# Two of a pack's four hat products moved from the second burst to the end of the first burst's turn, in a two-layer convolution kernel

## The chip, the core and the metric

The kernel runs on one core of one Trainium2 chip. A core has TensorE (PE in the profile; its weight loads are PEld), VectorE (DVE), ScalarE (ACT), GpSimd (POOL) and SyncE (SP), which here only issues DMAs. The metric is the device time of one execution in microseconds. Three executions of the kernel before gave 12756.01, 12768.52 and 12776.53 us; the median, 12768.52 us, is the time before.

## What is computed

The input is a batch of 32 images with 128 channels of 32 x 32 pixels. Layer 0 normalizes, encodes to 1024 channels, convolves along the flattened pixels, gates, normalizes and decodes. Layer 1 is a deformable depthwise convolution with 8 x 8 taps: a small depthwise convolution gives an offset for each tap and pixel, and the image is sampled there with bilinear weights.

```python
x = x + L0(_gn(x))            # h = u@W_enc; y = gelu(conv(h)); g = y@W_glu
                              # layernorm(h + g[:D]*sigmoid(g[D:])) @ W_dec
x = x + L1(_gn(x))
# L1, for each of 64 taps:
ix = px * sx - 0.5; iy = py * sy - 0.5
s = ((1-dx)*(1-dy))*gather(y0, x0) + (dx*(1-dy))*gather(y0, x0+1) \
  + ((1-dx)*dy)*gather(y0+1, x0) + (dx*dy)*gather(y0+1, x0+1)
acc = acc + s * w_t
# then batch norm and gelu
```

## The kernel before

A first stage makes the convolution of layer 0 for all images and leaves y in HBM. The main stage, `main_block`, then runs two generators side by side. `first_part(b)` does gate, values, normalization and decoding of layer 0 for one image, as two halves of 512 pixels with eight blocks m each: eight matmuls for the gate (L808), a sigmoid on ScalarE (L815), eight matmuls for the value (L831), the gating on VectorE (L839), one matmul of h (L847), a sum on VectorE (L860), its square on ScalarE (L868), and sums on GpSimd (L738, L869). `second_part(b)` does layer 1 for an image that is two behind. `run_along` merges them: it always advances the one that has done the smaller share of its cost, so that instructions of the two interleave in a fixed order on every engine. `prepare(b + 1)` is a list of steps with due times for the next image of layer 1 (normalization, depthwise taps, laying out of offsets in HBM), which `second_part` works off in `due(j)`: a step runs when its due time is at most three times the piece number plus j.

Bilinear sampling is done as a matmul. The hat function max(0, 1 - |t|) of an offset along x, times that along y, gives the weights of a small window of pixels (tile `s`, ds in the profile, 16 slots of 160 columns), and TensorE multiplies windows of the image (dxw) with them. An image has 17 packs of tap columns. For a pack h:

- the x hats of the whole image were made by `prepare` and stored in HBM; `load_x` brings those of a pack into one of two ds buffers (L1110), at the end of pack h - 2;
- the y offsets of a half pack come by `load_y` (L1125) into one of three dhy buffers, four DMAs in most packs;
- `hat_y(h, part)` makes the y hats of a quarter of a pack in place, two ScalarE instructions (L1145, L1146);
- `weights(h, part)` multiplies a quarter of ds by it on VectorE, 128 x 640 in most packs (L1151); after parts 1 and 3 it issues the `load_y` that reuses the buffer.

A pack's matmuls go in two bursts, pieces 0 and 1 (i = 0) and pieces 2 and 3 (i = 2), into four PSUM banks (dps, L1227). After each burst VectorE multiplies the banks by the tap weights into `prod`, one bank in each of four slots ("a turn", L1243), and at the end of the pack GpSimd adds up (L1269, L1275). A burst has six slots, which the `yield` lines bound: one after the matmuls, four with a bank each, one after `due(5)`. So a pack has twelve.

The products of pack h + 1 stand ahead of the second burst of pack h, and its hats in the first burst's turn. [...]SyncE's queue holds all loads of both streams: y of layer 0 (gy, L728), windows (dxw, L1166), the copies of `prepare` (L972, L984, L999, L1046), and those named above. `spread` (L984) copies offsets from HBM to HBM in runs of 20 values, four times an image.

Of the kernel before, what the change touches and what calls it, by code (L numbers as in the profile page):

```python
# [589 lines left out]
def main_block(nc, tc, const, ins, x, u_d, y_d, x1_d, out, offmax):  # L590
# [21 lines left out]
    with ctx:  # L612
# [459 lines left out]
        packs = [(b, us) for b in range(B) for _, us in PACKS]  # L1072
        s_of, hy_of, xw_of = {}, {}, {}

        def slots_of(n):
            return sum(span_of(u)[1] for u in PACKS[n][1])
# [56 lines left out]
        PARTS = 4  # L1133

        def cut_of(h, part):

            ends = ends_of(h)
            lo, hi, first = ends[part], ends[part + 1], ends[part - part % 2]
            t = hy_of[2 * h + part // 2]
            return slice(lo, hi), t[:, lo - first : hi - first]  # L1140

        def hat_y(h, part):

            t = cut_of(h, part)[1]
            nc.scalar.activation(t, t, AF.Abs, bias=minus_y)  # L1145
            nc.scalar.activation(t, t, AF.Relu, scale=-1.0, bias=const["one"])  # L1146

        def weights(h, part):

            cut, t = cut_of(h, part)  # L1150
            nc.vector.tensor_mul(s_of[h][:, cut], s_of[h][:, cut], t)  # L1151
            if part % 2:
                q = 2 * h + part // 2
                hy_of.pop(q)
                load_y(q + HB)
# [15 lines left out]
        def second_part(b, steps):  # L1171


            steps = sorted([*steps, *ending], key=lambda e: e[0])
            ending.clear()
            acc = one.tile([P, W, H], F32, tag="acc", name=f"dacc_{b}")
            nc.gpsimd.memset(acc, 0.0)
            for n in range(NP):
                x0, us = PACKS[n]
                m = slots_of(n)  # L1180
                xw = xw_of[b, x0]
                windows(b, n + 1)
                prod = prods[(b * NP + n) % 2]

                h = b * NP + n
                s = s_of.pop(h)

                for i in range(0, PIECES, 2):

                    def due(j):  # L1190
                        while steps and steps[0][0] <= 3 * (PIECES * n + i) + j:
                            steps.pop(0)[1]()

                    due(0)
                    work = []
                    if i > 0 and h + 1 < len(packs):
                        for part in range(PARTS):
                            weights(h + 1, part)
                    for piece in (i, i + 1):
                        ps = [  # L1200
                            psam.tile(
                                [P, 512], F32, tag="sam", name=f"dps_{b}_{n}_{piece}_{side}"
                            )
                            for side in range(2)
                        ]
                        lo = 0
                        for parts in zip(blocks_of(0, piece), blocks_of(1, piece)):
                            rows, run = parts[0][0][1], parts[0][0][3]
                            hi = lo + rows * run * m
                            to = [  # L1210
                                t[:, lo:hi].rearrange("p (s k v) -> p s k v", s=m, k=rows)
                                for t in ps
                            ]
                            for part in range(len(parts[0][1])):
                                for side in range(2):
                                    (ky, _, v0, _, step, skew), wins = parts[side]
                                    w, r0, r1 = wins[part]
                                    half = slice(64 * side, 64 * side + 64)
                                    frm = s[half, 0, ky * NV + v0 - VBASE[side] + r0 :]
                                    frm = bass.AP(  # L1220
                                        tensor=frm.tensor, offset=frm.offset,
                                        ap=[
                                            frm.ap[0], [CELLS, m],
                                            [step * NV + skew, rows], [1, r1 - r0],
                                        ],
                                    )
                                    nc.tensor.matmul(  # L1227
                                        to[side][:, :, :, r0:r1],
                                        xw[half, w, :], frm, start=True, stop=True,
                                    )  # L1230
                            for side in range(2):
                                work.append((piece, side, to[side], parts[side][0]))
                            lo = hi
                    yield measure(m)

                    def scale(piece, side):
                        for p, sd, frm, (ky, rows, v0, run, step, skew) in work:
                            if (p, sd) != (piece, side):
                                continue
                            wt = wk[:, table_of[n] : table_of[n] + m]  # L1240
                            wt = wt[:, :, ky : ky + step * (rows - 1) + 1 : step]
                            at_y = prod[:, ky * KS + v0 - ky :]
                            nc.vector.tensor_mul(  # L1243
                                bass.AP(
                                    tensor=at_y.tensor, offset=at_y.offset,
                                    ap=[
                                        at_y.ap[0], [H, m],
                                        [step * (KS - 1) + skew, rows], [1, run],
                                    ],
                                ),  # L1250
                                frm,
                                wt[:, :, :, None].to_broadcast([P, m, rows, run]),
                            )

                    for j in range(4):
                        due(1 + j)
                        scale(i + j // 2, j % 2)
                        if i == 0 and h + 1 < len(packs):
                            hat_y(h + 1, j)
                        yield measure(m)  # L1260
                    due(5)
                    yield measure(m)
                load_x(h + SB)

                def row(ky):
                    return prod[:, ky * KS : ky * KS + m * H]

                for to, frm in ((2, 0), (3, 1), (4, 6), (5, 7), (2, 4), (3, 5), (2, 3)):
                    nc.gpsimd.tensor_add(row(to), row(to), row(frm))  # L1269
                total = row(2)  # L1270
                slot = 0
                for u in us:
                    j0, nj = span_of(u)
                    to = acc[:, u - 7 + j0 : u - 7 + j0 + nj]
                    nc.gpsimd.tensor_add(  # L1275
                        to, to,
                        total[:, slot * H : (slot + nj) * H].rearrange(
                            "p (s y) -> p s y", y=H
                        ),
                    )  # L1280
                    slot += nj

            o = two.tile([P, L], F32, tag="img", name=f"do_{b}")
            xr = two.tile([P, L], F32, tag="img", name=f"dxr_{b}")
            nc.sync.dma_start(xr, x1_d[b])
            nc.gpsimd.tensor_scalar(  # L1286
                o.rearrange("p (h w) -> p w h", w=W), acc, bn_mean, bn_inv,
                op0=ALU.subtract, op1=ALU.mult,
            )
            ending.append((6, lambda: nc.scalar.activation(o, o, AF.Gelu, bias=bn_beta)))  # L1290
            ending.append((11, lambda: nc.vector.tensor_add(o, o, xr)))
            ending.append((14, lambda: nc.scalar.dma_start(out[b], o)))

        ending = []
        def measure(slots):

            return slots * 8.0 + 40.0
# [3 lines left out]
        def opening():  # L1301

            yield 30.0
            for _, step in prepare(0):
                step()
                yield 1.0
            for i in range(SB):
                load_x(i)
            for i in range(HB):
                load_y(i)  # L1310
            windows(0, 0)
            for part in range(PARTS):
                hat_y(0, part)
                weights(0, part)


        ctx.enter_context(tc.manual_schedule())
# [158 lines left out]
```

## Time and profile before

| what | value |
|---|---|
| time, median of three (lowest to highest) | 12768.52 us (12756.01 to 12776.53) |
| profiled execution: time, span | 12769.27 us, 12767.5 us |
| granted TensorE clock, mean | 0.972 |
| dps matmuls (L1227) | 23936 records, 2778.3 us busy |
| ds products (L1151) | 2176, 2821.2 us busy |
| y hats (L1145, L1146) | 2176 each, 1699.1 and 1726.5 us busy |
| dhy loads of 160 KB (L1125) | 3264 of about 4030 |
| ds loads of 400 KB or 480 KB (L1110) | 832 and 448 |

Times in the views are microseconds from the start of the span. A row of waits names the engine and line that waited, what ended the wait, the total, how often, and the longest. A row of the timeline gives start, duration, engine, line and operation, with "xN" for N instructions merged. The chain of waits is followed back from the end: each piece is the work that released the next one. Matmul records come in pairs: each matmul of 32-bit data shows as two.

### The profile page before, as it was taken

To read this page: it belongs to the slowest core of one execution; us is meant where nothing else is said; L and a number is where in the kernel's file an instruction comes from. 1 tells how busy PE (TensorE), PEld (TensorE's weight loads), DVE (VectorE), ACT (ScalarE), POOL (GpSimd) and SP (SyncE) were. 2 spreads that over 40 slices of the span, in tenths; PEclk is the share of its full clock that TensorE was granted. 3 is DMA by queue.
4 is the path that set the end of the run, shared out by engine and by line. 5 is a ranking of instruction groups with operands and counts; after the bars stand their busy time and mean duration, and the time that the engine had idled before them with its cause. 6 is when DMAs were issued, how large, how long until landed. Compare 5 with 4: busy or idle time off the path is not lost.

```text
span 12767.5 us, 157327 instructions
## 1 busy us (share of the span) xinstructions
PE 12216.4 (96%) x51362; PEld 6679.5 (52%) x51362; DVE 8277.2 (65%) x14315; ACT 5490.5 (43%) x7823; POOL 8094.1 (63%) x6987
## 2 busy tenths in 40 slices
PE   7999999999999999999999999999999999999965
PEld 7999444444444444444444444444444444444444
DVE  5555126666666667666666666666666666666667
ACT  4344124444444444444444444444444444444443
POOL 2555126666666676666666666667666666666668
PEclk9999999999999999999999999999999999999976
DMA  7899136666666666667666776666666667667666
GB/s 238 268 278 276 68 90 177 181 181 186 180 183 181 179 176 183 182 175 184 183 181 177 186 187 180 178 176 173 183 181 176 184 176 186 180 183 187 179 183 180
DMA packets 1521915, 2350.16 MB, mean 184 GB/s; under 512 B 619586, under 2 KB 835266, under 8 KB 1520066
## 3 DMA queue, kind: packets, MB, share of 16 engines
q1 hardware_dynamic: 1382210, 2027.97, 60.4%
q10 hardware_dynamic: 89728, 177.76, 3.8%
q0 software_dynamic: 49152, 134.28, 3.5%
q8 instruction: 413, 6.77, 0.2%
q14 instruction: 412, 3.38, 0.1%
HBM read 2016.61 MB, written 407.02 MB: 190 GB/s over the span
## 4 chain that ended last, share of the span: by engine, by line
PE 78%; DMA 7%; DVE 5%; POOL 3%; issue 2%; ACT 2%; SPq 2%; ACTq 0%; DVEq 0%; POOLq 0%
PE gpv L831 24%; PE gpg L808 23%; PE dps L1227 16%; PE psy L320 5%; PE psz L237 3%; DMA ds<-dhat 3%; PE gpo L736 3%; PE gph L847 3%; DVE ds L1151 2%; DVE prod L1243 2%; POOL prod L1269 1%; DMA dhy<-rel_d 1%; SPq L1125 1%; POOL do L1286 1%; DMA dxw<-dxw_d 1%
## 5 line engine op out<-in xcount | busy, mean ns | idle before, releaser
L1269 POOL TENSOR_TENSOR prod<-prod 128x512 f32<-128x512 f32 (+3 forms) x3808 | 4994.8, 1343 | 1614.0 <-DVE prod L1243 1571.4
L1243 DVE TENSOR_TENSOR prod<-dps,k_weight_slots 128x512 f32<-128x512 f32 (+16 forms) x8704 | 3126.1, 408 | 1437.5 <-PE dps L1227 1128.2
L808 PE MATMUL gpg<-gy,g_w_glu 128*128 128x512 f32 x8192 | 3771.8, 603 | 41.0 <-ACT gs L815 27.0
L831 PE MATMUL gpv<-gy,g_w_glu 128*128 128x512 f32 x8192 | 3751.7, 600 | 0.0
L1151 DVE TENSOR_TENSOR ds<-ds,dhy 128x640 f32<-128x640 f32 (+2 forms) x2176 | 2821.2, 1342 | 620.7 <-DMA ds<-dhat 354.8
L1227 PE MATMUL dps<-ds,dxw 64*128 64x128 f32 (+14 forms) x23936 | 2778.3, 375 | 364.4 <-DVE prod L1243 329.5
L1227 PEld LDWEIGHTS dps<-ds,dxw 64*128 64x128 f32 x23936 | 1979.9, 197 | 1455.5 <-DVE prod L1243 560.5
L808 PEld LDWEIGHTS gpg<-gy,g_w_glu 128*128 128x128 f32 x8192 | 1522.7, 191 | 1965.0 <-issue 1910.6
L831 PEld LDWEIGHTS gpv<-gy,g_w_glu 128*128 128x128 f32 x8192 | 1514.0, 190 | 1887.3 <-issue 1887.3
L869 POOL TENSOR_TENSOR gs<-gs,gq 128x512 f32<-128x512 f32 x448 | 647.2, 1445 | 2257.2 <-ACT gq L868 2257.2
L1145 ACT ACTIVATE dhy<-dhy,k_minus_y 128x640 f32<-128x640 f32 (+2 forms) x2176 | 1699.1, 781 | 532.5 <-DMA dhy<-rel_d 197.7
L1146 ACT ACTIVATE dhy<-dhy,one 128x640 f32<-128x640 f32 (+2 forms) x2176 | 1726.5, 793 | 71.1
L868 ACT ACTIVATE gq<-gr 128x512 f32<-128x512 f32 x448 | 281.4, 628 | 2556.9 <-DVE gr L860 2555.6
L839 DVE SCALAR_TENSOR_TENSOR gs<-gpv,k_b_glu,gs 128x512 f32<-128x512 f32 x512 | 384.2, 750 | 1374.8 <-PE gpv L831 1296.9
L815 ACT ACTIVATE gs<-gpg,k_b_glu 128x512 f32<-128x512 f32 x512 | 351.6, 687 | 1867.3 <-PE gpg L808 1722.0
L1275 POOL TENSOR_TENSOR dacc<-dacc,prod 128x256 f32<-128x256 f32 (+6 forms) x1184 | 1048.1, 885 | 92.8
L357 POOL DMA_DIRECT2D y_d<-yo x1024 | 590.0, 583 | 690.6 <-ACT yo L344 641.2
L320 PE MATMUL psy<-toe,z 128*128 128x192 f32 x4096 | 668.0, 326 | 7.4 <-DVE z L242 5.5
L320 PEld LDWEIGHTS psy<-toe,z 128*128 128x128 f32 x4096 | 663.3, 196 | 11.4 <-DVE z L242 6.8
L738 POOL TENSOR_TENSOR gs<-gs,gr 128x512 f32<-128x512 f32 x448 | 652.3, 1456 | 0.0
L335 DVE TENSOR_TENSOR psy<-psy,t 128x256 f32<-128x256 f32 (+2 forms) x768 | 333.8, 435 | 345.9 <-ACT t L328 329.1
L847 PE MATMUL gph<-gu,k_W_enc 128*128 128x512 f32 x1024 | 522.9, 592 | 0.0
(164 smaller groups left out, 6046.8 us busy)
## 6 DMA issues: line engine op xcount, KB each, us to landing
dhy<-rel_d SPq DMA_DIRECT2D x3264, 160.0 KB
ds<-dhat SPq DMA_DIRECT2D x832, 400.0 KB
ds<-dhat SPq DMA_DIRECT2D x448, 480.0 KB
dxw<-dxw_d SPq DMA_DIRECT2D x832, 224.0 KB
y_d<-yo POOLq DMA_DIRECT2D x1024, 128.0 KB, 4.1
gy<-y_d SPq DMA_DIRECT2D x512, 256.0 KB
u<-u_d SPq DMA_DIRECT2D x224, 512.0 KB
dhat<-dh ACTq DMA_DIRECT2D x256, 390.0 KB
```

What stands on the lines that cost most here:

```text
L320: nc.tensor.matmul(ps[:, c // 2, c % 2, :], rows[i][:, (g * CG + c0 + c) // 2, c % 2, :], toe[:, c0 + c, :], start=True, stop=True,)
L738: nc.gpsimd.tensor_add(sums[0], sums[0], r)
L808: nc.tensor.matmul(gate, w_glu[:, k, D + m * P : D + m * P + P], ys[k], start=(k == 0), stop=(k == KD - 1),)
L831: nc.tensor.matmul(val, w_glu[:, k, m * P : m * P + P], ys[k], start=(k == 0), stop=(k == KD - 1),)
L847: nc.tensor.matmul(h, w_enc[:, m * P : (m + 1) * P], u, start=True, stop=True)
L1145: nc.scalar.activation(t, t, AF.Abs, bias=minus_y)
L1146: nc.scalar.activation(t, t, AF.Relu, scale=-1.0, bias=const["one"])
L1151: nc.vector.tensor_mul(s_of[h][:, cut], s_of[h][:, cut], t)
L1227: nc.tensor.matmul(to[side][:, :, :, r0:r1], xw[half, w, :], frm, start=True, stop=True,)
L1243: nc.vector.tensor_mul(bass.AP(tensor=at_y.tensor, offset=at_y.offset, ap=[at_y.ap[0], [H, m], [step * (KS - 1) + skew, rows], [1, run],], ...
L1269: nc.gpsimd.tensor_add(row(to), row(to), row(frm))
L1275: nc.gpsimd.tensor_add(to, to, total[:, slot * H : (slot + nj) * H].rearrange("p (s y) -> p s y", y=H),)
```

## The change

Products 0 and 1 of pack h + 1 stand at the end of the first burst's turn in pack h, after `due(5)` and ahead of the last slot; products 2 and 3 stay ahead of the second burst. Hats 2 and 3 of pack h + 1 go into the first two slots with a bank of the first turn, and hats 0 and 1 of pack h + 2 into the same slots of the second turn. The opening makes hats 0 and 1 of pack 1 too. As `weights(h + 1, 1)` issues a `load_y`, that load moves with it.

```diff
                     due(0)
                     work = []
                     if i > 0 and h + 1 < len(packs):
-                        for part in range(PARTS):
-                            weights(h + 1, part)
+                        weights(h + 1, 2)
+                        weights(h + 1, 3)
                     for piece in (i, i + 1):
...
                     for j in range(4):
                         due(1 + j)
                         scale(i + j // 2, j % 2)
-                        if i == 0 and h + 1 < len(packs):
-                            hat_y(h + 1, j)
+                        if j < 2 and h + 1 + i // 2 < len(packs):
+                            hat_y(h + 1 + i // 2, (2, 0)[i // 2] + j)
                         yield measure(m)
                     due(5)
+                    if i == 0 and h + 1 < len(packs):
+                        weights(h + 1, 0)
+                        weights(h + 1, 1)
                     yield measure(m)
                 load_x(h + SB)
...
             for part in range(PARTS):
                 hat_y(0, part)
                 weights(0, part)
+            for part in range(2):
+                hat_y(1, part)
```

## The prediction

> **What bounds the kernel now.** I read four views of the profile, from coarse to fine. First, busy time by stretch: the convolution stage, the main stage in which both parts of the block run together, and the tail in which the last two images have the deformable part alone (rows: stretch and length, then busy us of PE, PEld, DVE, ACT, POOL, the granted clock, DMA share, GB/s).
>
> ```profile
> PE 12216.4 (96%) x51362; PEld 6679.5 (52%) x51362; DVE 8277.2 (65%) x14315; ACT 5490.5 (43%) x7823; POOL 8094.1 (63%) x6987
> ...
> 1853.00:12212.00 10359.00, 10223.34 (x40281) 5058.19 (x40281) 7059.68 (x12082) 4625.43 (x6177) 7002.17 (x5563) 0.99 0.68 180
> 12212.00:12767.00 555.00, 291.08 (x1555) 219.87 (x1553) 395.44 (x716) 232.04 (x300) 417.25 (x336) 0.64 0.69 187
> ```
>
> In the main stage TensorE stands still for 10359.0 - 10223.3 = 135.7 us, over 30 images 4.5 us each. That is all a better order can win there, with some clock: 0.99 instead of 1.00 is about 1% of 10223, another 100 us. The tail is 555 us, and TensorE is busy for 291 of it. Second, who ended TensorE's waits, in these two stretches (us, times, longest):
>
> ```profile
> PE dps L1227 <- DVE prod L1243: 124.1, 88, 7.2
> PE dps L1227 <- DMA dhy<-rel_d: 6.9, 1, 6.9
> PE dps L1227 <- DMA dxw<-dxw_d: 4.7, 1, 4.7
> ...
> PE dps L1227 <- DVE prod L1243: 205.4, 36, 18.5
> ```
>
> So it is always a burst's bank that VectorE has not yet read out. Third, VectorE's own waits in the main stage: what holds it where it should make the next pack's weights (ds)?
>
> ```profile
> DVE ds L1151 <- DMA ds<-dhat: 289.7, 148, 6.5
> DVE do L1291 <- ACT do L1290: 170.9, 29, 6.3
> DVE ds L1151 <- ACT dhy L1146: 168.1, 97, 2.9
> ...
> DVE gn_r L917 <- ACT gn_r L914: 90.2, 30, 3.0
> ```
>
> Fourth, one image's stalls. There are two that count. One of about 0.7 us (5076.6 to 5077.3, say) is VectorE at its limit among the depthwise taps: 19.2 of 20 us busy. The other comes 54 us later, in packs 8 and 9, and takes 1.2 to 7.2 us. Here it is in the chain of waits, 6157 to 6177 us:
>
> ```profile
> 6157.54 5.57 DMA dhy<-rel_d
> 6163.10 0.02 issue
> 6163.12 8.90 DMA ds<-dhat
> 6172.02 0.03 DVEq L1151
> ...
> 6172.84 0.82 DVE ds L1151
> 6173.66 0.35 DVE prod L1243
> 6174.01 0.04 issue
> 6174.05 3.48 PE dps L1227 x24
> 6177.53 3.03 PE gpg L808 x4
> ```
>
> TensorE's first burst of pack 9 waits for a bank; VectorE has the products of pack 9's weights ahead of the evictions, and these wait for the last piece of the load into ds. That load was issued late because SyncE and the DMA engines were at the spreads (rel_d, 80-byte runs):
>
> ```profile
> 6139.47 10.36 SPq L984 DMA_DIRECT2D rel_d<-rel_n  x3
> 6149.93 8.85 SPq L1125 DMA_DIRECT2D dhy<-rel_d  x8
> 6158.87 2.68 SPq L728 DMA_DIRECT2D gy<-y_d  x4
> 6161.82 1.83 SPq L1110 DMA_DIRECT2D ds<-dhat  x3
> ```
>
> From 6140 to 6174 the DMA share is 0.97. The end of the stall is the landing of the third piece (6172.02), two products of 0.82 and an eviction. In the tail it is a loop through the same load: products, dhy loads, ds load, landing, about 14.1 us a pack (products of successive packs start at 12570.84, 12585.30 and 12599.11).
>
> **What the Trainium skill says.** "PSUM — Partial Sum Buffer", section Engine vs sequencer instructions: the queues of ScalarE, VectorE and GpSimd are strictly first in, first out. The trace fits: VectorE ends its sum (L860) at 5020.50 and then sits 3.03 us before L917, with products behind it whose load had landed. So what matters is which neighbours an instruction passes. "SBUF — State Buffer", Who interferes with whom: a VectorE instruction with two SBUF inputs contends with a GpSimd one that reads SBUF. A 128x640 product takes 1.361 us on average but 0.82 in the stall, where GpSimd waits too; moving products doesn't take that cost off. "DMA: Bandwidth & Descriptors", Issuing engines are not separate DMA queues: all DMAs end on the same 16 engines; only the issuing time differs by place. In the window above this decides. "TensorE: Matmul & The Clock Gate", What's actually happening: an idle array is throttled and must be busy again before it runs at full rate. Here, after 2.34 us of idling, four gate records took 3.03 us instead of 1.72, so an idle us costs about another.
>
> **The change, part by part.** I laid the instruction sequences of the two programs side by side.
>
> TensorE and GpSimd: no instruction changes place. Nothing is added or dropped on any engine: 2176 products, 2176 pairs of hat functions, the same loads.
>
> VectorE: the move sounds large and is small. Between the end of the first turn and the second burst lies one slot of the other stream. An image has 17 x 12 = 204 slots beside 292 matmul slots, so 1.43 matmuls a slot; eight records take 3.43 us, two records a matmul, so 0.86 us each and 1.2 us a slot. A VectorE instruction of the other stream rarely falls into it. In fact only 61 pairs of products pass anything: 31 pass L917/L918 (pack 3) and 30 pass L860 (pack 8), so two places an image.
> - Pack 3: VectorE waited 90.2/30 = 3.0 us for ACT's square root; two products, 2 x 1.36 = 2.7 us, now fill it. TensorE was busy 20.00 of 20 us there, and VectorE had caught up by 5035.09, where it waits 0.82 us for TensorE. Worth 0 in the main stage, at best 30 x 0.7 = 21 us if the following stall went with it.
> - Pack 8: in the old order L860 runs at 6165.21, and the products start at 6168.48 and 6170.09. In the new one the second product ends at 6170.92, L860 until 6171.67, still before the third piece lands at 6172.02. Worth 0; if it doesn't fit, 0.75 x 30 = 22 us lost. Behind L860 wait ACT's square (L868) and GpSimd's sums; the matmuls that need these (L736 at 6180.40, the mean's later) are not reached.
>
> ScalarE: the hat pairs keep their own sequence, parts 0, 1, 2, 3 pack after pack. Parts 0 and 1 move six slots earlier against the sigmoids and squares, parts 2 and 3 two slots. A pair is 0.817 + 0.829 = 1.65 us. VectorE's 168.1 us of waiting for hats should nearly vanish, but it is not where TensorE stalls (packs 8 and 9 wait for the load), so I cost it at 0. What covers it is TensorE's other work; without that it would be up to 168 us. The earlier places of parts 2 and 3 ask for their dhy load 2 slots sooner: normally it is issued at 5001.5 and used after 5012; in pack 8 ScalarE will wait some 2 us, with L868 as the next instruction and its input later still. 0 again.
>
> SyncE: in each pack four dhy loads go out one slot earlier. In sequence they pass one window copy (L1046) twice an image, one gy load, and, in pack 7, the last of the four spreads. The last is the place that counts. The spread now goes behind four dhy issues of 0.64 us, 2.6 us. The four move from behind to before it, so all from the fifth dhy on stands behind the same work as before. With the DMA share at 0.97 I expect the ds load to land at the same time: 0. Bounds: 2.6 us later, if issuing decides, and 1 us earlier, as the last dhy load need not wait for the spread (at 10321.56 it did so for 1.0 us). Both are per image and count twice for the clock.
>
> The tail: order as before but for image 31's preparation. The two products before L917 save about 3 us of its chain (products started at 12288.44, behind L918 and a hat that is gone from that place), and the ds load after the spreads is issued perhaps 2 us sooner. -5 us. The opening does two hat pairs more, 3.3 us, under image 1's matmuls, and pack 0 does them less: 0.
>
> Sum: 0 + 0 + 0 + 0 - 5 = -5 us against the profiled execution's 12769.27 us (span 12767.5), which is 0.8 us over the median of the three runs. So 12764 us: no change that can be measured (0.2%, 26 us, is what I take as the bound).
>
> **The rivals.**
> - A, faster: the congested stretch drains sooner. For it: small and large runs get mixed, and the digits of DMA share between 6147 and 6158 fall to 0.6, so the DMA engines are not full while spreads are generated. Against: the total is the same and the ds load keeps its place. If the load lands 1 us sooner: 30 x 1 x 2 = 60, 12709 us.
> - B, slower: SyncE becomes what decides in pack 7. The four dhy loads wait for VectorE's second product, and the last spread, all other loads and the ds load wait behind. It decides once the ds load's issue slips more than the queue hides: by the semaphore updates in the trace, a piece of ds takes 6.5 us (median) from issue to landing, 3.9 at least, so 2.6 us. I price half the upper bound: 30 x 1.3 x 2 = 78, 12847 us. Against: the slip equals the cover at worst.
> - C: hats that wait for dhy hold a sigmoid (L815), and TensorE runs out of its three gate banks. For it: in the main stage L839 waited 60.3 us behind hats already. 30 x 0.7 = 21 us, 12790.
>
> **How the numbers follow.** Forecast 0.58, A 0.26, B 0.11, C 0.05. The forecast's own range, 12742 to 12790, has both pack places' bounds. To leave out no more than 2 in 10 I reach over A's middle and to C: 12705 to 12800. Faster: A's greater part and a little of the forecast, 0.25; slower: B and part of C, 0.15; same 0.60.
>
> **What would show it.** Right: VectorE's wait for hats under 40 us, that for ACT in L917 near 0, TensorE's idle time in the main stage still 120 to 150 us, the pack 9 stall ending with a ds landing. Wrong: that stall gone or doubled, the ds load issued over 2 us later after the spreads, or waits of L808 and L831 for ACT.

## The result, and the profile after

| | before | after |
|---|---|---|
| median (lowest to highest), 20 runs each on one chip | 12767.22 us (12750.74 to 12780.0) | 12787.56 us (12769.97 to 12802.37) |
| ratio, 95% interval | | 1.0017 (1.001 to 1.0024) |
| profiled execution: time, span | 12769.27, 12767.5 us | 12774.51, 12772.8 us |

The change made the kernel slower by about 20 us, 0.17%, where -5 us had been forecast. The profiled execution of the changed kernel is one of the quickest of its twenty, so its trace shows only 5 us of that. In the text below "before" and "after" are these two traces.

Busy time by stretch, of after, for the main stage and the tail (columns as in the prediction):

```profile
1853.00:12212.00 10359.00, 10224.28 (x40285) 5066.05 (x40283) 7073.43 (x12072) 4630.81 (x6172) 6973.98 (x5559) 0.99 0.69 180
12212.00:12767.00 555.00, 296.14 (x1568) 226.17 (x1564) 405.10 (x727) 232.83 (x302) 420.88 (x340) 0.63 0.70 187
```

Taken alone this says that nothing happened: TensorE stands still for 10359.0 - 10224.3 = 134.7 us, against 135.7. TensorE's waits of after in the main stage:

```profile
PE dps L1227 <- DVE prod L1243: 96.8, 53, 6.7
PE dps L1227 <- DMA dhy<-rel_d: 34.1, 6, 7.4
```

The sum is 130.9 us (135.7 in three rows before), but there are 59 waits where there were 90. The short ones are gone and the long ones are longer. VectorE's waits of after, in the same stretch:

```profile
DVE ds L1151 <- DMA ds<-dhat: 255.3, 135, 7.0
...
DVE ds L1151 <- ACT dhy L1146: 6.5, 6, 2.0
```

The wait for y hats went from 168.1 us to 6.5, and the one in L917 (90.2 us) no longer appears. Next the place where TensorE stalls, in the same image as the prediction's stall at 6172 us; in after it comes some 14 us later in the span. This is the timeline of after there, first VectorE (start, duration, instruction, and in brackets the idle time before it), then GpSimd:

```profile
6182.79 0.82 DVE L1151 TENSOR_TENSOR ds<-ds,dhy 128x640 f32<-128x640 f32 x1 [4.18 <-DMA ds<-dhat]
6184.48 0.83 DVE L1151 TENSOR_TENSOR ds<-ds,dhy 128x640 f32<-128x640 f32 x1 [0.86 <-DMA ds<-dhat]
6185.22 0.75 DVE L860 SCALAR_TENSOR_TENSOR gr<-gph,k_b_enc,gs 128x512 f32<-128x512 f32 x1
6186.87 2.52 DVE L1151 TENSOR_TENSOR ds<-ds,dhy 128x640 f32<-128x640 f32 x2 [0.91 <-ACT gq L868]
```

```profile
6186.71 1.27 POOL L869 TENSOR_TENSOR gs<-gs,gq 128x512 f32<-128x512 f32 x1 [9.47 <-ACT gq L868]
```

This is the new thing. The third piece of ds landed at 6186.79 (by the semaphore updates in the trace). The last pair of products starts 0.08 us later, and its row takes 2.52 us. In before the row of the same pair takes 1.56 us (VectorE, then GpSimd):

```profile
6165.21 0.75 DVE L860 SCALAR_TENSOR_TENSOR gr<-gph,k_b_enc,gs 128x512 f32<-128x512 f32 x1
...
6172.10 1.56 DVE L1151 TENSOR_TENSOR ds<-ds,dhy 128x640 f32<-128x640 f32 x2 [1.19 <-DMA ds<-dhat]
```

```profile
6166.70 1.26 POOL L869 TENSOR_TENSOR gs<-gs,gq 128x512 f32<-128x512 f32 x1 [2.97 <-ACT gq L868]
```

GpSimd adds a square to its sum here (L869). In before this addition is over at 6167.96, ahead of all four products; in after it falls into the 2.52 us. It does so because L860 now stands behind the first pair of products and runs later: L860 releases ScalarE's square (L868), and that releases the addition, 1.49 us after L860 began. The bracket on the last row names ScalarE, but the product waited for the load; the square merely ended at about the same time. The chain of waits of after errs in the same way:

```profile
6179.13 9.45 DMA gy<-y_d
...
6188.58 0.81 DVE ds L1151
6189.39 0.34 DVE prod L1243
...
6189.78 4.95 PE dps L1227 x24
```

It sees only the last product and credits the time before it to whatever transfer ended nearest, a gy load that no product needs. A product that runs slowly looks like a wait for something else; its duration in the timeline tells the truth. The last row has a second lesson, taken up below: 24 records took 4.95 us, where the same group in before's chain took 3.48.

SyncE's issues of after in this image (start, time, line, transfer):

```profile
6152.52 7.14 SPq L984 DMA_DIRECT2D rel_d<-rel_n  x2
6161.98 3.96 SPq L1125 DMA_DIRECT2D dhy<-rel_d  x4
6165.98 0.59 SPq L984 DMA_DIRECT2D rel_d<-rel_n  x1
6166.67 5.67 SPq L1125 DMA_DIRECT2D dhy<-rel_d  x4
...
6174.90 2.83 SPq L1110 DMA_DIRECT2D ds<-dhat  x3
```

The last spread stands between the two groups of dhy loads now, as the diff says. To see what this adds up to I took means over images from the traces, each image counted from its first gate matmul (L808) to that of the next:

| mean over 29 images, us | before | after |
|---|---|---|
| short stall at the depthwise taps | 0.79 | 0.18 |
| first spread issued | 141.83 | 140.69 |
| last spread issued | 153.51 | 158.26 |
| third ds piece lands | 180.53 | 179.18 |
| end of the long stall | 182.58 | 182.11 |
| landing to end of stall | 2.05 | 2.93 |
| long stall | 3.50 | 4.22 |

The landing comes 1.35 us earlier, and 0.88 us of that is lost between landing and matmul.

### The profile page after: what moved, and what is told of

It reads as the page before. It is cut to its first block, busy times and chain, and to the rows that moved or that the text cites. A ratio compares the mean times of both kernels' runs of the same rounds, so it can differ in the third digit from the quotient of the medians.

```text
span 12772.8 us, 157357 instructions
## 1 busy us (share of the span) xinstructions
PE 12217.9 (96%) x51362; PEld 6691.2 (52%) x51362; DVE 8298.8 (65%) x14315; ACT 5499.2 (43%) x7823; POOL 8069.5 (63%) x6987
## 4 chain that ended last, share of the span: by engine, by line
PE 72%; DVE 9%; DMA 9%; issue 3%; POOL 3%; SPq 3%; ACT 1%; ACTq 0%; DVEq 0%; POOLq 0%
PE gpv L831 23%; PE gpg L808 21%; PE dps L1227 15%; PE psy L320 5%; DVE ds L1151 4%; PE psz L237 3%; DMA ds<-dhat 3%; PE gpo L736 3%; PE gph L847 3%; DVE prod L1243 2%; DMA dxw<-dxw_d 2%; DMA dhy<-rel_d 2%; POOL prod L1272 1%; SPq L1125 1%; POOL do L1289 1%
## 5 line engine op out<-in xcount | busy, mean ns | idle before, releaser
L808 PE MATMUL gpg<-gy,g_w_glu 128*128 128x512 f32 x8192 | 3775.1, 604 | 43.7 <-ACT gs L815 29.3
L1151 DVE TENSOR_TENSOR ds<-ds,dhy 128x640 f32<-128x640 f32 (+2 forms) x2176 | 2882.0, 1375 | 410.9 <-DMA ds<-dhat 321.7
L808 PEld LDWEIGHTS gpg<-gy,g_w_glu 128*128 128x128 f32 x8192 | 1523.0, 191 | 1971.6 <-issue 1901.3
L869 POOL TENSOR_TENSOR gs<-gs,gq 128x512 f32<-128x512 f32 x448 | 659.9, 1473 | 2327.8 <-ACT gq L868 2327.7
L868 ACT ACTIVATE gq<-gr 128x512 f32<-128x512 f32 x448 | 281.4, 628 | 2857.3 <-DVE gr L860 2856.1
L839 DVE SCALAR_TENSOR_TENSOR gs<-gpv,k_b_glu,gs 128x512 f32<-128x512 f32 x512 | 384.2, 750 | 1468.1 <-PE gpv L831 1448.4
L847 PE MATMUL gph<-gu,k_W_enc 128*128 128x512 f32 x1024 | 522.9, 592 | 0.0
```

Of the source, the lines that this page charges most:

```text
L808: nc.tensor.matmul(gate, w_glu[:, k, D + m * P : D + m * P + P], ys[k], start=(k == 0), stop=(k == KD - 1),)
L847: nc.tensor.matmul(h, w_enc[:, m * P : (m + 1) * P], u, start=True, stop=True)
L869: nc.gpsimd.tensor_add(sums[1], sums[1], sq)
```

## The experiments

Theory P (port): pack 3's fill is worth something, as everything up to the ds landing comes over 1 us earlier, and pack 8's move costs about 0.9 us an image, because it sends GpSimd's sum into the pair of products that ends the stall. "The pair" below is these last two products of pack 9, after the third piece has landed; its times are means over images that count each product alone (1.65 us in before, 2.52 in after). Rivals: S, SyncE's order in pack 7 makes the load late; H, ScalarE's hats are in the way; G, the chain of loads gives back whatever VectorE gains. The experiments ran on four chips, A to D, and on A and B all kernels are some 90 us slower than on the chip of the result. Each ratio is against runs of the kernel before on the same chip.

**Chip A (kernel before: 12859.65 us).** The changed kernel again:

> The changed kernel once more, for a second trace. P (GpSimd in the way): in the traces so far VectorE's two products after the last ds piece has landed take 1.65 us together before the change and 2.52 us after it, because GpSimd's sum L869, which the sum L860 sets off, now runs beside them. P expects the same here: 2.3 to 2.7 us for the pair, the end of the stall 2.9 us after the landing (2.05 before the change), stall near 4.2 us an image or longer, stall of the depthwise taps near 0.2 us; time 1.0017 of before. S (SyncE's order in pack 7) expects instead that the ds load of pack 9 lands later after the first spread than before the change (38.7 us): 39 us or more in a run as slow as the median. H (ScalarE's hats) expects waits of TensorE or VectorE on ScalarE that weren't there.

12852.77 us, ratio 0.9998 (0.9990 to 1.0006). The pair took 2.56 us, and the stall ended 2.97 us after the landing, as P says. The ratio that I expected was missed: on this chip the change costs nothing. That became the second question.

Pack 8 left as it was:

```diff
-                        weights(h + 1, 2)
-                        weights(h + 1, 3)
+                        for part in range((0 if n == 8 else 2), PARTS):
+                            weights(h + 1, part)
...
-                        weights(h + 1, 0)
-                        weights(h + 1, 1)
+                        for part in range((0 if n == 8 else 2)):
+                            weights(h + 1, part)
```

> The change in every pack but pack 8, where all four products stay ahead of the second burst, so that L860 is ahead of them again. P: the pair of products back at 1.65 us, end of the stall 2.05 us after the landing; the landing stays early (1.3 us earlier in the image than before the change, from pack 3). Some 0.9 us an image less than the changed kernel, and with the clock 27 to 42 us: 0.9985 to 1.0000 of before, the stall near 3.3 us. S and H: nothing but pack 8's order has changed, so as the changed kernel, 1.0017, stall 4.2 us.

12829.63 us, 0.9977 (0.9970 to 0.9984), 23 us less than the changed kernel. Pair 1.65 us, end of stall 2.05 us after the landing. S and H are against this: nothing of theirs, pack 7's issues and the hats, was touched.

The kernel before with pack 3 alone, and with pack 8 alone (the edit of the first; the second has 8 in place of 3). In both the hats stay where they were, and the load of y offsets that product 1 issues moves with it in that pack:

```diff
-                        for part in range(PARTS):
+                        for part in range((2 if n == 3 else 0), PARTS):
                             weights(h + 1, part)
...
                     due(5)
+                    if i == 0 and h + 1 < len(packs):
+                        for part in range((2 if n == 3 else 0)):
+                            weights(h + 1, part)
```

> The kernel before with two products moved in pack 3 alone (they fill VectorE's wait ahead of L917); hats, loads and all other packs as before. P: the taps' stall falls from 0.8 to 0.2 us, the first spread and the ds landing come 1.1 to 1.35 us earlier in the image, the pair stays at 1.65 us, the stall is 2.7 to 3.5 us; 10 to 60 us faster, 0.9955 to 0.9990. A theory that the load's chain gives back whatever VectorE gains (G) expects the landing where it was and the stall longer by 0.6 us: 0.999 to 1.002.

12833.51 us, 0.9983 (0.9976 to 0.9991). The taps' stall fell to 0.17 us, and the ds landing came at 181.40 us in the image, against 182.50 in the kernel before (this from chip B, equally slow). G falls.

> The kernel before with two products moved in pack 8 alone, ahead of L860. P: landing and taps' stall as before (38.7 us after the first spread, 0.8 us), the pair 2.3 to 2.7 us, end of the stall 2.9 us after the landing, stall 4.2 to 4.5 us; 26 to 42 us slower, 1.0020 to 1.0033. S and H, as well as G: 1.000, since neither SyncE's order in pack 7 nor the hats nor pack 3 have changed.

12889.77 us, 1.0026 (1.0016 to 1.0037). The landing is that of the kernel before (182.49), the pair takes 2.63 us, the stall ends 3.04 us after the landing. So two places of the change do all that matters, -0.17% and +0.26%, with opposite signs.

**Chip B (12858.18 us).** What is it in pack 8: the wait, the order, or GpSimd?

> The kernel before once more, for a trace on the same chip as the next three. 1.000. Its stall of the depthwise taps 0.8 us an image, the pair of products after the landing 1.65 us, end of the stall 2.05 us after the landing. P (the port story: pack 8's move lets GpSimd's sum run into the pair) and S (SyncE's order) say the same of it; it gives the landing that S needs for comparison.

> The changed kernel on the same chip. P: the gain of pack 3 (landing 1.1 to 1.35 us earlier in the image) and the loss of pack 8 (0.9 us between landing and end of the stall) nearly cancel, so 0.9995 to 1.0017, as the two measurements so far. S: the landing counted from the first spread is later than in the kernel before by 0.3 us or more, and that is the loss: 1.0017.

Before: 12863.41 us, 1.0004 (0.9996 to 1.0013). After: 12854.37 us, 0.9998 (0.9989 to 1.0006). Landing, counted from the first spread: 40.71 us in one, 40.74 in the other; on the chip of the result, 38.70 and 38.49. S needed 0.3 more.

```diff
                 hy_of.pop(q)
-                load_y(q + HB)
+                if part > 1 or h == 0:
+                    load_y(q + HB)
...
                     if i > 0 and h + 1 < len(packs):
+                        load_y(2 * (h + 1) + HB)
                         weights(h + 1, 2)
```

> The changed kernel, but the load of y offsets that moved with product 1 is issued where it was, ahead of the second burst; on all other engines as the changed kernel. P: pair, landing and time as the changed kernel within 0.0007. S: the last spread goes out 5 us earlier again, the landing with it by 0.3 us or more, and the time falls by 0.0008 to 0.002 against the changed kernel.

12860.91 us, 1.0001 (0.9993 to 1.0009). The last spread is issued 6.7 us earlier in the image (153.15 instead of 159.81), and the landing is at 181.37 instead of 181.44. S falls: the order of these issues does not move the ds load.

```diff
-                        nc.gpsimd.tensor_add(sums[1], sums[1], sq)
+                        if (hf, m) != (0, 7):
+                            nc.gpsimd.tensor_add(sums[1], sums[1], sq)
```

> The changed kernel without one of GpSimd's additions an image: the square of block 7 of the first half is not added to the sum of squares (L869), so the normalization of that half uses too small a variance. ScalarE's square and L860 stay in their place. P: nothing runs on GpSimd beside the pair, so 1.65 us again, end of the stall 2.05 us after the landing, and 0.002 to 0.0033 faster than the changed kernel, 0.997 to 0.9990 of before. If it is L860's own 0.75 us on VectorE, or the place of the products, that costs, as I priced it before: as the changed kernel, within 0.0007.

12826.22 us, 0.9976 (0.9966 to 0.9986): 28 us less than the changed kernel, all orders kept, one addition of GpSimd's an image left out. The timeline of VectorE in this kernel at one such stall, where GpSimd does nothing from 5157.05 to 5170.74 (line numbers from L869 on are one higher here):

```profile
5165.45 0.74 DVE L860 SCALAR_TENSOR_TENSOR gr<-gph,k_b_enc,gs 128x512 f32<-128x512 f32 x1
5167.18 1.56 DVE L1152 TENSOR_TENSOR ds<-ds,dhy 128x640 f32<-128x640 f32 x2 [0.99 <-ACT gq L868]
```

L860 stands in the same place and costs nothing; the last two products take 1.56 us together again (1.65 by the mean over images). This is the direct test of P: the cost is GpSimd's addition beside the products, not L860's 0.75 us.

**Chip C (12787.47 us).** Can the stall itself be taken away, and do the hats matter?

```diff
-                *((81 + 3 * i, spread(i // 2, i % 2)) for i in range(4)),
-                (99, gather), *((109 + 9 * k, hat(k)) for k in range(8)),
+                *(((81, 84, 96, 99)[i], spread(i // 2, i % 2)) for i in range(4)),
+                (111, gather), *((119 + 8 * k, hat(k)) for k in range(8)),
```

> The kernel before with two of the four spreads taken out of the crowd: due times 81, 84, 96, 99 in place of 81, 84, 87, 90, the gather at 111 and the x hats from 119 in steps of 8, so that the load of ds for pack 9 goes out between the two pairs. If the landing of that load is all that the long stall waits for, the stall of packs 8 and 9 goes or falls below 2 us: 3.5 to 5.4 us an image and up to 2.5 us of slower running after it, 100 to 240 us, 0.981 to 0.992 of before. If the load is late for another reason, or the same crowd comes one pack later, 0.997 to 1.003.

> The changed kernel with the same split of the spreads. P: without the stall, GpSimd's sum beside the pair costs nothing any more, since the pair is not what TensorE waits for; so within 0.002 of the kernel before with the split, or faster by what pack 3 brings (0.7 us an image, 0.0017). If the change costs by its order alone (loads, hats), it stays behind that kernel by 0.001 or more.

> The changed kernel with the spreads still further apart: 81, 87, 97, 103, the gather at 113, x hats from 120 in steps of 8. If two spreads side by side are still too many, this is faster than the split into pairs, by up to 0.003; if the load only needs to be out of the way of the last two, the same within 0.001.

Before with the split: 12787.8 us, 0.9998 (0.9990 to 1.0007), far from the 0.981 to 0.992 that I hoped for, and inside the range given for the same crowd one pack later. TensorE's waits in the main stage say why:

```profile
PE gph L847 <- DVE gs L839: 133.9, 30, 6.4
PE dps L1227 <- DVE prod L1243: 31.9, 62, 1.5
```

The long stall has moved to the h matmul (L847), where VectorE's L839 is stuck behind products that wait for the next pack's load. The changed kernel with the split ran 12753.75 us, 0.9972 (0.9963 to 0.9982), and with the wider split 12757.72 us, 0.9972 (0.9961 to 0.9983). So with the stall moved elsewhere the same change is a gain of 34 us, about 0.27%, and not a loss. That is more than the 0.17% that I put down to pack 3; in the traces TensorE waits 27 us less at L847 too (106.5 against 133.9), and why was not taken apart. That the change costs anything is a matter of one meeting in one pack.

All four products of every pack back ahead of the second burst, with only the hats left moved:

```diff
-                        weights(h + 1, 2)
-                        weights(h + 1, 3)
+                        for part in range(0, PARTS):
+                            weights(h + 1, part)
...
-                        weights(h + 1, 0)
-                        weights(h + 1, 1)
+                        for part in range(0):
+                            weights(h + 1, part)
```

> The changed kernel with all four products of every pack ahead of the second burst, as before the change: of the change only ScalarE's hats have moved (and the two in the opening). P: landing, pair and stalls as in the kernel before, 0.9993 to 1.0007. H: the hats' new places alone cost what the change cost on the first chip, 1.0010 to 1.0024.

12776.83 us, 0.9993 (0.9985 to 1.0002): no loss from the hats. H falls. (The "first chip" of the expectation is the chip of the result. The changed kernel itself did not run on chip C; d3_not8 below, with the hats moved and a gain where the changed kernel loses, says the same.)

**Chip D (12762.06 us).** Why does the same kernel lose 0.17% on one chip and nothing on two others? K: the running after the stall costs more once the stall is long.

> The kernel before, for its stall on this chip. K: the time from the end of the stall to the next image is 164 us in images with a stall over 3 us, 162.5 or less below that, whatever the kernel. 1.000.

> The changed kernel on the same chip. K: if the stall of the kernel before is 3 to 4 us here, the time after the stall is 0.3 to 0.6 us longer than in the kernel before and the ratio 1.0005 to 1.0020; if it is 5 us or more, the same time after the stall within 0.2 us and a ratio of 0.999 to 1.0006.

> The change without pack 8. P: 0.0015 to 0.0030 below the changed kernel wherever it runs.

Before: 12764.06 us, 1.0000 (0.9992 to 1.0008). After: 12786.22 us, 1.0019 (1.0012 to 1.0026): the loss is back. After without pack 8: 12749.65 us, 0.9989 (0.9982 to 0.9995), 0.0030 below. The granted clock shows what happens. Two stalls of the kernel before, from d1_before by stretch (columns as above; the third number from the end is the clock): one of 4.8 us and the 6 us behind it, then one of 2.3 us and the 6 us behind it.

```profile
4106.60:4111.40 4.80, 0.02 (x2) 0.01 (x1) 2.72 (x4) 0.00 (x0) 0.00 (x0) 0.96 1.05 234
4111.40:4117.40 6.00, 6.00 (x30) 4.70 (x31) 4.28 (x15) 2.36 (x3) 4.32 (x7) 0.50 0.79 197
...
4453.70:4456.00 2.30, 0.03 (x1) 0.00 (x1) 1.90 (x3) 0.00 (x0) 0.00 (x0) 1.00 1.00 277
4456.00:4462.00 6.00, 6.00 (x35) 3.68 (x36) 4.58 (x15) 3.48 (x5) 4.31 (x7) 1.00 1.06 268
```

After the long stall TensorE runs at half clock for the 6 us shown; after the short one at full clock. The time from the end of the stall to the next image shows it: 161.2 us at full clock, 162.6 to 165 otherwise. An image "escapes" if its clock stays full after the stall. Images that escape, and an image's time in three parts:

| traces | images with full clock after the stall | image start to stall, us | stall | stall to next image |
|---|---|---|---|---|
| before and d1_before | 17 of 58 | 178.92 | 3.44 | 163.00 |
| after and d2_after | 2 of 58 | 177.84 | 4.24 | 163.85 |
| d3_not8 | 1 of 29 | 177.83 | 3.28 | 163.77 |
| b1_before (chip B) | 0 of 29 | 179.12 | 5.42 | 163.95 |
| b2_after (chip B) | 0 of 29 | 177.88 | 6.49 | 164.00 |

On the chip of the result and on chip D the change gives -1.08 + 0.80 + 0.85 = +0.57 us an image, 17 us over 30 images, beside some 20 measured. On chip B no image escapes in either kernel, and -1.24 + 1.07 + 0.05 = -0.12 us is left, 4 us less. This is a reading of traces; no experiment held the clock fixed. K is right in that the slowing is what differs, but not in its sizes: on chip D the time after the stall rose from 162.86 to 164.07 us, 1.2 us where K gave 0.3 to 0.6. Nor is its threshold right: from 3 us on none of the 98 stalls of the first three rows escapes, but below that 17 of 27 do in the kernel before, 2 of 8 in the changed one and 1 of 12 in d3_not8.

What decides below 3 us is mostly when the stall begins. In the records of these traces the granted clock changes only at points that lie whole steps of 3.413 us apart, and after a stall it is low for one, two or three such steps (four once). Of these 47 short stalls, 24 began between 0.38 and 0.77 of a step, and 20 of them escaped; 23 began elsewhere in the step, and none escaped. In the kernel before 20 of 27 began in the good part, in the changed one 3 of 8, in d3_not8 1 of 12. So the changed kernel lost its escapes mostly by length (8 of 58 stalls below 3 us, where before had 27 of 58); d3_not8, with 12 of 29, lost them by where its stalls begin. What draws the limits of the good part stays open.

> The changed kernel with one spread a pack, right behind the loads of ds and of the windows (due times 84, 96, 108, 120), the gather at 128, x hats from 134 in steps of 6. If what makes the loads late is two spreads in a row, the stalls of TensorE fall to below 1.5 us an image and the time by 100 us or more, 0.986 to 0.992 of before; if a single spread is enough to hold the loads behind it, four stalls of 1 us or so take the place of one, 0.995 to 1.005.

```diff
-                *((81 + 3 * i, spread(i // 2, i % 2)) for i in range(4)),
-                (99, gather), *((109 + 9 * k, hat(k)) for k in range(8)),
+                *(((84, 96, 108, 120)[i], spread(i // 2, i % 2)) for i in range(4)),
+                (128, gather), *((134 + 6 * k, hat(k)) for k in range(8)),
```

12593.61 us, 0.9867 (0.9852 to 0.9882): the best version, ahead of the kernel before by 168 us and of the changed one by 193. TensorE's two largest waits in its main stage, and that stage by stretch:

```profile
PE dps L1227 <- DVE prod L1243: 34.3, 38, 7.3
PE gph L847 <- DVE gs L839: 10.1, 12, 1.4
```

```profile
1853.00:12040.00 10187.00, 10157.67 (x40312) 5010.52 (x40311) 7052.48 (x12087) 4640.65 (x6178) 6999.53 (x5568) 1.00 0.70 184
```

TensorE stands still for 29.3 us in place of 134.7, and the clock is 1.00. The experiment changes both the number of spreads in a pack and their place behind its loads; which of the two does it was not tried apart.

## Why the prediction was wrong

The range held the time, but the forecast was -5 us, nothing that can be measured, and the measured change was +20 us, clear of the noise. All the signs named for "right" came: a wait for hats of 6.5 us, none left in L917, 134.7 us of idle time, a stall that ends with a ds landing. They are sums over the main stage, in which a gain and a loss nearly cancel; that so much fitted is luck. By its steps:

- **Pack 8, "worth 0; if it doesn't fit, 0.75 x 30 = 22 us lost".** This is the step that failed. L860 did fit: it ended before the third piece landed, as predicted. But the step priced the products behind it at 0.82 us, the duration they had while "GpSimd waits too". The step itself noted that GpSimd's sums wait behind L860; putting L860 off until just before that landing set them free at just that moment. They meet because the landings of the second and third piece are about 2.3 us apart: a product (0.83), L860 (0.75) and the square (0.63) nearly fill this, and the addition starts as the last pair does. Measured: 0.88 us an image, +0.26% alone; with pack 8 left out the loss is gone on chip D (0.9989 instead of 1.0019).
- **Pack 3, "worth 0 in the main stage, at best 21 us".** The upper bound was about right, the value taken was not. The following stall did go (0.79 to 0.18 us), and the first spread and the ds landing came over 1 us earlier. Alone it gives -0.17%, 22 us (26 by the medians). The reason for 0, that VectorE had caught up at its next wait for TensorE, overlooked that it fell behind again at the taps.
- **SyncE, "I expect the ds load to land at the same time: 0".** Right, by b3_oldload. What rival B feared did not occur.
- **ScalarE, 0.** Right: the waits for hats are gone, and c4_hats shows no loss and no gain clear of the noise. Rival C did not occur.
- **"An idle us costs about another".** The reading itself was too high: four records that took 3.03 us instead of 1.72 are 1.31 us for 2.34 us of idling. The Trainium skill, "TensorE: Matmul & The Clock Gate", section What's actually happening, knows two states of the clock, full and half, and a window of 3.4 us that runs free of the kernel, in which the array's activity is judged. The traces agree with both: the states are 1.00 and 0.50, and the changes lie whole steps of 3.413 us apart. So the cost is not proportional to the idle time: it is nothing, or on average 1.4, 2.6 or 3.6 us for one, two or three steps at half clock, so equal sums of idle time (135.7 and 134.7 us) cost differently. A stall below 3 us escapes or not by where it begins in such a step. By the sum above, this mis-sized term makes the loss on the chip of the result; without it pack 3 and pack 8 nearly cancel (-1.08 + 0.80 us an image).
- **The tail, -5.** TensorE's last gate matmul ended 554.3 us before the end in before and 555.1 in after: nothing.
- **Rival A** priced the landing 1 us sooner at -60 us. The landing did come sooner, by way of pack 3, and 0.88 of its 1.35 us was spent before TensorE saw it.

"SBUF — State Buffer", Who interferes with whom, was cited in the prediction for this very conflict, to say that moving products doesn't remove it. The page calls the shared port an exclusive lock, and the trace agrees: in the timeline above the addition ends at 6187.98 and the first of the two products 0.68 us later, nearly its whole 0.82 us. What was missing was the question whether the move creates the conflict.

## What to carry to other kernels

When an instruction is moved past another, follow what the passed one releases on the other engines, and lay that beside the new critical instructions: a duration read while a neighbour was idle holds only as long as the neighbour stays idle. A stall that a transfer ends is worth treating at the transfer: here four HBM-to-HBM copies, set one to a pack, brought 1.3%, while all reordering of the vector work moved 0.3%. Where the granted clock drops after stalls, count the stalls that it drops after, not the sum of idle time.

## What the runs showed of the hardware

- A 128x640 product on VectorE takes 0.82 us alone and up to 1.94 us when a 128x512 addition of GpSimd runs beside it: it waits for the addition rather than sharing with it. In after 149 products met just one such addition that had begun before them, and in the median they ended 0.68 us after it; 10 began before the addition and took 0.82 to 0.83 us, and the addition was the one that took longer, 1.46 to 1.86 us instead of 1.27.
- After a stall TensorE's granted clock was 0.50 for a whole number of steps of 3.413 us, mostly two, or not lowered at all. Of the stalls of the kernel before on the chip of the result and chip D, 8 of 10 below 2 us escaped, 9 of 17 between 2 and 3 us, and none of 31 above; where in such a step a short stall began decided most of it.
- Chips differ in how fast these copies and loads go: in the kernel before and in a4_only8 the ds piece landed at 182.5 us in the image on chips A and B, and at 180.1 to 180.5 on chip D and that of the result. The stall and the running after it were 2.9 us an image longer there, 88 of some 92 us by which the kernel was slower, and the 0.17% loss by the change was not seen (0.9998).
- With two of the four spreads put off to the next pack, the stall only moved by a pack; with one a pack, right behind the pack's loads, it was all but gone.
